# Within a step: node products behind the tasks, node sums behind the weighing, tasks sorted by the age of their inputs

## The chip, the core and the metric

The kernel runs on one core of a Trainium2 chip. A core has five engines with an instruction row each: TensorE (PE, with weight loads PEld), VectorE (DVE), ScalarE (ACT), GpSimd (POOL) and SyncE (SP, which here only issues DMAs). The metric is the device time of a run in microseconds; less is better. The kernel before took 2186.42 us, the median of three runs (2183.76 to 2202.97).

## What is computed

A graph attention layer and a mixture of experts, each added to its input. `x` has 6250 nodes of 256 features, there are 100000 edges, sorted by destination, with destinations denser at low node numbers.

```python
x = x + gnn(layernorm(x), src, dst, ...)      # 8 heads of 32
x = x + moe(layernorm(x), ...)                # 8 experts, the 2 best for each node

# gnn, after a layer norm
h     = xn @ W
e     = leaky_relu(a_src[src] + a_dst[dst], 0.2)
ee    = exp(e - emax[dst])
alpha = ee / segment_sum(ee, dst)[dst]
agg   = segment_sum(h[src] * alpha, dst)
o     = layernorm(agg + xn @ W_res + bias)
return o + gelu_tanh(o @ ffn_w1 + b1) @ ffn_w2 + b2

# moe
top_p, top_idx = top_k(softmax(x @ Wr + br), 2)
y[e] = gelu(layernorm_e(x) @ W1[e] + b1[e]) @ W2[e] + b2[e]
return sum over the two experts of weight * y[expert]
```

## The kernel before

After a first part (to about 150 us) that makes a table `tab_s` of `h` and its attention factors, the kernel runs in **steps**, one loop (L1481 and after) that traces everything by hand: `tc.manual_schedule()` keeps each engine's instructions in the order in which the program emits them. An engine takes its row in that order; what it waits for is a semaphore of another engine or of a DMA.

A step does two things. First it runs the **edge stages** of `STAGES` (L910). Every step `s` fetches four tiles of 128 edges, and the later stages of the pipeline work on what was fetched in earlier steps; a pair `(f, d)` in `STAGES` calls `f(s - d)`:

- `spread` (d=0, DVE, L821 and L828): one-hot of each edge's place in a window of 32 nodes, and the factors `qd`; `turn_spread` (1, PE and ACT, L834, L836) transposes it through the PSUM tile `pt`; `give` (2, PE, L842) gathers destination factors into `pz`.
- `weigh` (3, DVE, L850 to L854): weights and weighted messages `msg` from the gathered `gs` and `pz`; it frees `gs` for the next gathers on POOL (`fetch`, d=0, L812).
- `add_tiles` (4, PE, L869): one-hot times messages, summed in PSUM over a group of steps in `pl`; at the group's end ACT copies it to `part` (L873).
- `place` (4, DVE, L887): at a group's end, a one-hot `oh2` (two buffers) that moves the group's sums to their nodes.
- `add_nodes` (5, PE, L894): the product for nodes, `p2 = oh2 x part`, in a PSUM tile with one buffer (the trace shows it as `p`).
- `sum_up` (6, DVE, L901 and L905): adds `p2` to the nodes' sums `acc_lo` or `acc_hi`, at a place that DVE first loads into a register (`kfi`).

A group has one step in the first 66 steps, where there are few edges for each node, then two steps (31 groups), four (9) and eight (4): 110 groups in 196 steps.

Then the step runs **tasks** (`run_tasks`, L937): pieces of the rest of the work, for units of two node tiles and for blocks of 256 rows of one expert, chosen while each engine has `room` in the step. A task names its engine and its inputs; an input made by another engine must be at least one step old. The PSUM tile `py` has one buffer: a task with `take="py"` can be chosen only when it is free, and a task with `free="py"` chosen earlier in the same step frees it. The tasks spoken of below:

- first units: `wres` (`first_product`, PE, L1147, takes `py`); `rg` (`add_biases`, DVE, L1153 and L1156, frees it).
- node units: `divide` (DVE, L1036 to L1041; its input is an SP load) and `norm_out` (DVE, to L1051); `norm_rows` (ACT); `turn` (PE, L966, through `pt`, and ACT, L973); eight `up` (PE, L981, and ACT, L984); four `down` (PE, L991; the first takes `py`); `add_out` (DVE, L1064); `take_up` (DVE, L1071, frees `py`); `norm_new` (DVE, to L1087); a second `turn`; `logits` (PE, L1113, takes `py`); `choose` (DVE, L1121, frees it).
- for every two units: `mark`, `append`, `rank` (DVE, L1281 to L1296, frees the `py` that `count` took), `enlist`, and scatters (POOL, L1351).
- expert blocks: loads (SP), `note` (DVE, L1417; waits for a buffer that a give-back's DMA has read), `turn`, `up`, `down`, `finish` (DVE, L1426, frees `py`), `weigh_block` (ACT, L1432), give-backs (POOL, L1436).

What a step emits on an engine is thus: the edge stages in the order of `STAGES`, then the tasks in the order in which they were chosen.

Of the kernel before, what the change touches and what calls it, by code (L numbers as in the profile page):

```python
# [218 lines left out]
def gnn_moe_kernel(  # L219
# [47 lines left out]
    while EP < ET:  # L267
        m = 8
        while m > 1:
            gap = 2.0 * N * min(NE, (EP + G * m) * P) / NE ** 2  # L270
# [15 lines left out]
    NG = len(order)  # L286
# [161 lines left out]
    with ExitStack() as actx:  # L448
# [229 lines left out]
        for t0 in range(0, NT, G):  # L678
# [15 lines left out]
            for j in range(n):  # L694
                t = t0 + j
# [91 lines left out]
    def fetch_nodes(c):  # L787

        gq = bw.tile([P, W32 * 2 * H], F32, name="gq", bufs=1)
        nc.gpsimd.indirect_dma_start(  # L790
            out=gq, out_offset=None, in_=tab_q,
            in_offset=bass.IndirectOffsetOnAxis(ap=qrow[:, c:c + 1], axis=0))
        nc.sync.dma_start(tab_g[c * P:(c + 1) * P, :], gq)
        n = min(GC, NQ - c * GC)
        gd = bw.tile([P, GC, 2 * H], F32, name="gd")
        nc.sync.dma_start(gd[:, :n], tab_g[c * P:c * P + n * G, :].rearrange(
            "(g j) (r c) -> (j r) g c", j=G, r=W32))
        gds[c] = gd
# [91 lines left out]
    @behind_group  # L890
    def add_nodes(q):
        part, oh2 = live.pop((q, "part")), live.pop((q, "oh2"))
        p2 = bps.tile([P, DA], F32, name="p2")
        nc.tensor.matmul(p2, oh2, part, start=True, stop=True)  # L894
        live[q, "p2"] = p2

    @behind_group
    def sum_up(q):
# [4 lines left out]
        for b in range(2):  # L903
# [3 lines left out]

    STAGES = ((sum_up, 6), (weigh, 3), (add_tiles, 4), (place, 4), (turn_spread, 1), (give, 2),  # L910
              (spread, 0), (add_nodes, 5), (fetch, 0))
    LASTST = 6


    class Task:
# [3 lines left out]
        def __init__(self, fn, eng, cost, deps=(), take=None, free=None):  # L919
            self.fn, self.eng, self.cost, self.take, self.free = fn, eng, cost, take, free  # L920
            self.deps = []
            for d in deps:
                d, gap = d if isinstance(d, tuple) else (d, None)
                if gap is None:
                    gap = 0 if d.eng == eng == "DVE" else 1
                self.deps.append((d, gap))
            self.step = None

    pending = []
    held = set()  # L930

    def task(*a, **k):
        t = Task(*a, **k)
        pending.append(t)
        return t

    def run_tasks(s, room):  # L937

        more = True
        while more:  # L940
            more = False
            for t in list(pending):
                if (t.take in held or room[t.eng] <= 0.0
                        or any(d.step is None or d.step + gap > s for d, gap in t.deps)):
                    continue
                pending.remove(t)
                t.step = s
                room[t.eng] -= t.cost
                if t.take:
                    held.add(t.take)  # L950
                if t.free:
                    held.remove(t.free)
                t.fn()
                more = True

    def back(tasks, n):

        return tasks[-n:][:1] if len(tasks) >= n else []
# [208 lines left out]
    def first_unit(u):  # L1167
        t0, n, _ = units[u]
        env = {}
        first_loads.append(task(lambda: load_first(t0, n, env), "SP", 0.0,  # L1170
                                [(d, 0) for d in back(firsts, 2)]))
        pr = task(lambda: first_product(n, env), "PE", 0.95 * n, [(first_loads[-1], 2)], take="py")
        ab = task(lambda: add_biases(n, env), "DVE", 0.7 * n,
                  [pr, *[(d, 0) for d in back(firsts, 1)]], free="py")
        firsts.append(task(lambda: store_first(t0, n, env), "SP", 0.0, [ab]))
# [265 lines left out]
    def block_loads(b):  # L1441
        env = {"n": 2}
        needs = next(d for n, d in sure if n > b)
        free = [(d, 0) for d in blocks[b - 2:b - 1] + notes[b - 2:b - 1]] if b >= 2 else []
        env["lw"] = task(lambda: load_weights(b, env), "SP", 0.0,
                         [needs[-1], *([blocks[b - 2]] if b >= 2 else [])])
        env["lx"] = task(lambda: load_block(b, env), "SP", 0.0, [*needs, *free])
        env["lp"] = task(lambda: load_params(b, env), "DVE", 0.4, [needs[-1], *free])
        ahead.append((b, env))

    def block_unit(b, env):
        no = task(lambda: note(b, env), "DVE", 0.6,
                  [(env["lx"], 2), *[(d, 0) for d in back(stored, 3)]])
        dn = net(env, lambda: env["xb"], [(env["lx"], 2), env["lp"]], lambda: env["w"][0],
                 lambda: env["w"][1], AF.Gelu, lambda: env["pc"][:, 0, :],
                 more=[(env["lw"], 2)], scale=lambda: env["pc"][:, 0, KF:])
        fi = task(lambda: finish(env), "DVE", 0.7, [dn, *[(d, 0) for d in back(stored, 2)]],
                  free="py")
        wb_ = task(lambda: weigh_block(env), "ACT", 0.9, [fi, no])
        g0 = task(lambda: give_back(0, env), "POOL", 2.6, [wb_])  # L1460
        stored.append(task(lambda: give_back(1, env), "POOL", 2.6, [g0]))
        blocks.append(fi)
        notes.append(no)
# [15 lines left out]
    s, u, since, was_nodes = 0, 0, [], False  # L1479

    with tc.manual_schedule():  # L1481
        nc.sync.dma_start(xs[E * CAP:, :].rearrange("(p r) d -> p r d", r=2), blank[:, :2])
        while s < NG + LASTST or pending or u < len(units) or len(blocks) < NS:
            for g in range(s, min(s + EARLY, NG)):
                if order[g][0] // GC not in gds:
                    fetch_nodes(order[g][0] // GC)
            for f, d in STAGES:
                if 0 <= s - d < NG:
                    f(s - d)
            if s == NG + LASTST:  # L1490
                edges.close()
            if len(firsts) < len(units) and len(firsts) <= s + 1:
                first_unit(len(firsts))
            if len(firsts) == len(units) and firsts[-1].step is not None and fp:
                first_.close()
                fp = None
            if last_hi and last_hi[0].step is not None and not moew and not fp:
                hi_pool.close()
                moew.append(ctx.enter_context(tc.tile_pool(name="moew", bufs=2, side="right")))
            nb = len(blocks) + len(ahead)  # L1500
            if moew and len(ahead) < 2 and nb < NS and any(n > nb for n, _ in sure):
                block_loads(nb)

            while sum(t.cost for t in pending if t.eng == "PE") < QUEUE:
                if (u < len(units) and units[u][2] <= s - LASTST
                        and not (ahead and was_nodes)):
                    was_nodes = True
                    node_unit(u)
                    since.append(u)
                    u += 1  # L1510
                    if u % 2 == 0 or u == len(units):
                        chunk_tasks(since, u == len(units), u == len(units) - 1)
                        since = []
                elif ahead:
                    was_nodes = False
                    block_unit(*ahead.pop(0))
                else:
                    break
            room = dict(ROOM if s < NG + LASTST else ROOM_AFTER)
            if s < NG + LASTST:  # L1520
                g = s - 5
                ends = 0 <= g < NG and order[g][1] == groups[order[g][0]][1] - 1
                for e in EDGES:
                    room[e] -= EDGES[e] + ends * BEHIND[e]
            run_tasks(s, room)
            s += 1
            if there is None and final_list and final_list[0].step is not None and len(blocks) > NS - 2:
                there = nc.values_load(total[0:1, 0:1], min_val=0, max_val=NB)
        if NS < NB:
            with tc.If(there > NS):  # L1530
                while pending or len(blocks) < NB:
                    nb = len(blocks) + len(ahead)
                    if len(ahead) < 2 and nb < NB:
                        block_loads(nb)
                    if ahead:
                        block_unit(*ahead.pop(0))
                    run_tasks(s, dict(ROOM_AFTER))
                    s += 1
# [31 lines left out]
```

## Time and profile before

| | |
|---|---|
| median of the timed runs | 2186.42 us |
| the profiled execution's own time | 1972.14 us |
| its span, first to last instruction | 1970.4 us |
| mean granted TensorE clock | 0.926 |
| busy: PE, PEld | 1634.8 us (83%), 1250.6 us (63%) |
| busy: DVE, ACT, POOL | 1078.1 us (55%), 707.7 us (36%), 1122.1 us (57%) |
| L894, 220 matmuls (two for each product) | 84.3 us busy, 59.5 us idle of PE before them |
| L905, 220 sums (two for each group) | 108.3 us busy, 106.2 us idle of DVE before them |
| L812, 784 gathers on POOL | 809.9 us busy, 363.9 us idle before them |

Times are those of one profiled execution, which was shorter than the timed runs; durations below are its own. "Busy" is the sum of the instructions' own times; "idle before" is how long the engine stood still just before such an instruction, put down to what ended the wait. A name behind an arrow is the one that was waited for; "issue" means that nothing visible was waited for. A matmul in fp32 appears as two.

### The profile page before, as it was taken

Reading aid. Unit: us, or ns where it says so; the run is one execution under the profiler, and the core shown is the slowest. Engines: PE = TensorE matmul, PEld = TensorE weight load, DVE = VectorE, ACT = ScalarE, POOL = GpSimd, SP = SyncE. Lnnn points to the kernel's source line nnn. Section 1 sums busy time; section 2 is a strip of 40 time slices with the busy share of each in tenths; the row PEclk is TensorE's granted clock in tenths of the full one; section 3 lists DMA queues with packets and bytes.
Section 4 is the critical chain, followed back from the end, with each engine's and each line's share of the span. In section 5 each row is a group of like instructions: output and inputs, shape, how many; then the busy total and the mean of one; then the engine's idle time right before and its main releaser. Section 6 shows DMA issues by size and latency. Waiting matters only on the chain. (4 is left out here: it accounts for less than half of the span.)

```text
span 1970.4 us, 28382 instructions
## 1 busy us (share of the span) xinstructions
PE 1634.8 (83%) x8533; PEld 1250.6 (63%) x8533; DVE 1078.1 (55%) x3964; ACT 707.7 (36%) x1590; POOL 1122.1 (57%) x1165
## 2 busy tenths in 40 slices
PE   4835797778787988999899997996998949999997
PEld 3523565555555766766677765775776737777775
DVE  8836878877878775565667655462453501200000
ACT  3821232322233343344434342433334314333332
POOL 2027765655655767577778777777777722112122
PEclk8968899887887999999999998998999979999999
DMA  4967664644535456566564776576776655565652
GB/s 129 290 210 225 187 202 130 184 134 146 158 112 194 152 152 170 149 199 168 179 200 136 210 206 200 155 220 201 201 232 169 205 184 131 179 186 171 196 161 57
DMA packets 245260, 348.24 MB, mean 177 GB/s; under 512 B 46465, under 2 KB 200353, under 8 KB 245100
## 3 DMA queue, kind: packets, MB, share of 16 engines
q1 hardware_dynamic: 182476, 203.56, 31.8%
q0 software_dynamic: 59312, 139.32, 27.1%
q10 hardware_dynamic: 3312, 3.48, 0.6%
q8 instruction: 70, 1.15, 0.2%
q14 instruction: 90, 0.74, 0.1%
HBM read 282.90 MB, written 67.66 MB: 178 GB/s over the span
## 5 line engine op out<-in xcount | busy, mean ns | idle before, releaser
L812 POOL DMA_INDIRECT gs<-tab_s,srce x784 | 809.9, 1033 | 363.9 <-issue 198.9
L981 PE MATMUL ph<-turned_in,w1b 128*128 128x256 f32 x1696 | 400.3, 390 | 51.2 <-ACT ht L984 38.2
L991 PE MATMUL py<-w2b,ht 128*128 128x256 f32 x1696 | 382.6, 384 | 11.7 <-DVE lg L1121 6.2
L981 PEld LDWEIGHTS ph<-turned_in,w1b 128*128 128x128 f32 x1696 | 305.2, 193 | 124.4 <-ACT ht L984 57.4
L991 PEld LDWEIGHTS py<-w2b,ht 128*128 128x128 f32 x1696 | 325.0, 193 | 58.4 <-DVE lg L1121 7.7
L1436 POOL DMA_INDIRECT out_dram<-yb,to x106 | 176.9, 1668 | 312.5 <-ACT yb L1432 124.5
L984 ACT ACTIVATE ht<-ph,pc 128x256 f32<-128x256 f32 x424 | 198.4, 473 | 206.1 <-PE ph L981 205.6
L854 DVE TENSOR_TENSOR msg<-gs,msg 128x1024 f32<-128x1024 f32 x196 | 240.5, 1227 | 6.7
L1426 DVE TENSOR_TENSOR yb<-py,b2b 128x512 f32<-128x512 f32 x53 | 36.6, 690 | 360.4 <-PE py L991 276.8
L991 PE MATMUL py<-w_sb,ht 128*128 128x256 f32 x784 | 190.5, 405 | 17.3 <-DVE lg L1121 15.0
L981 PE MATMUL ph<-turned_in,w_sb 128*128 128x256 f32 (+1 forms) x800 | 192.5, 394 | 14.2 <-ACT ht L984 14.2
L991 PEld LDWEIGHTS py<-w_sb,ht 128*128 128x128 f32 x784 | 158.7, 205 | 46.4 <-DVE lg L1121 19.6
L981 PEld LDWEIGHTS ph<-turned_in,w_sb 128*128 128x128 f32 x800 | 150.4, 200 | 44.6 <-ACT ht L984 20.3
L873 ACT ACTIVATE part<-pl 128x264 f32<-128x264 f32 x110 | 42.9, 390 | 322.3 <-PE pl L869 319.6
L836 ACT ACTIVATE oht<-pt 128x128 f32<-128x128 f32 x196 | 53.9, 275 | 271.5 <-PE pt L834 214.8
L869 PE MATMUL pl<-msg,oh 128*32 128x264 f32 x1568 | 130.9, 406 | 17.1 <-DVE msg L854 17.0
L1351 POOL DMA_INDIRECT xs<-xe,slot x98 | 103.4, 1055 | 54.3 <-DMA xs<-blank 22.1
L894 PE MATMUL p<-part,oh 128*128 128x264 f32 x220 | 84.3, 469 | 59.5 <-DVE acc_hi L905 38.8
L984 ACT ACTIVATE ht<-ph,prm 128x256 f32<-128x256 f32 (+1 forms) x200 | 92.2, 469 | 113.0 <-PE ph L981 112.6
L834 PEld LDWEIGHTS pt<-ident,oh 128*128 128x128 f32 x196 | 27.6, 141 | 138.3 <-issue 81.0
L834 PE MATMUL pt<-ident,oh 128*128 128x128 f32 x196 | 65.5, 334 | 49.6 <-ACT turned_in L973 23.1
L973 ACT ACTIVATE turned_in<-pt,pc 128x256 f32<-128x256 f32 x106 | 53.9, 559 | 134.4 <-PE pt L966 124.1
(325 smaller groups left out, 1900.8 us busy)
## 6 DMA issues: line engine op xcount, KB each, us to landing
w1b<-in_L_ffn_W_dram SPq DMA_DIRECT2D x53, 1024.0 KB
w2b<-in_L_ffn_W_dram SPq DMA_DIRECT2D x53, 1024.0 KB
xb<-xs SPq DMA_DIRECT2D x53, 260.0 KB
gs<-tab_s,srce POOLq DMA_INDIRECT x784, 3.3
b2b<-in_L_ffn_b_dram SPq DMA_DIRECT2D x53, 128.0 KB
tab_s<-hg SPq DMA_DIRECT2D x12, 544.0 KB
xg<-in_x_dram SPq DMA_DIRECT2D x12, 512.0 KB
xt_d<-xt SPq DMA_DIRECT2D x12, 512.0 KB
```

The lines of the kernel that those rows point to most:

```text
L812: nc.gpsimd.indirect_dma_start(out=gs[:, j, :], out_offset=None, in_=tab_s, in_offset=bass.IndirectOffsetOnAxis(ap=srce[:, t:t + 1], axis=0))
L834: nc.tensor.transpose(po[:, 0, :P], live[s, "oh"].rearrange("p j r -> p (j r)"), ident)
L836: nc.scalar.activation(oht, po[:, 0, :P], AF.Copy)
L854: nc.vector.tensor_tensor(msg[:, :, :D].rearrange("p t (h d) -> p t h d", h=H), gs[:, :, :D].rearrange("p t (h d) -> p t h d", h=H), msg[: ...
L869: nc.tensor.matmul(pl[j * W32:(j + 1) * W32, :], oh[:, j, :], msg[:, j, :], start=i == 0, stop=last)
L894: nc.tensor.matmul(p2, oh2, part, start=True, stop=True)
L973: nc.scalar.activation(xt[:, k, :n * P], pt[:, k, :n * P], AF.Identity, bias=scale[:, KD + k:KD + k + 1], scale=scale[:, k:k + 1])
L981: nc.tensor.matmul(ph[:, :W], w1[:, k, c * P:(c + 1) * P], env["in"][:, k, :W], start=k == 0, stop=k == KD - 1)
L984: nc.scalar.activation(ht[:, :W], ph[:, :W], func, bias=b[:, c:c + 1], scale=1.0)
L991: nc.tensor.matmul(env["py"][:, j, :], env["ht", c][:, j * P:(j + 1) * P], w2[:, c, :], start=c == 0, stop=c == KF - 1)
L1351: st = nc.gpsimd.indirect_dma_start(out=xs, out_offset=bass.IndirectOffsetOnAxis(ap=slots[k][:n, t:t + 1], axis=0), in_=xes[u // 2][:n, pl ...
L1436: nc.gpsimd.indirect_dma_start(out=out, out_offset=bass.IndirectOffsetOnAxis(ap=env["to"][:, j:j + 1], axis=0), in_=env["yb"][:, j, :], in ...
```

## The change

Three edits, all in what a step emits in which order. No instruction is added or taken away by them.

1. `STAGES` no longer has `add_nodes`; the loop calls `add_nodes(s - 5)` after the step's tasks.
2. `sum_up` moves from the head of `STAGES` to behind `spread`.
3. `run_tasks` still chooses tasks in the same way, but emits them only when all are chosen, sorted by `late`: 0 for a task without an input from the last step (an SP load never counts), 1 for a task with one. A task takes over the `late` of an input of the same step, and of the task that freed the PSUM tile that it takes, if that was in the same step. The sort keeps the order of equals.

```diff
-    STAGES = ((sum_up, 6), (weigh, 3), (add_tiles, 4), (place, 4), (turn_spread, 1), (give, 2),
-              (spread, 0), (add_nodes, 5), (fetch, 0))
+
+    STAGES = ((weigh, 3), (add_tiles, 4), (place, 4), (turn_spread, 1), (give, 2), (spread, 0),
+              (sum_up, 6), (fetch, 0))
     LASTST = 6
...
             self.step = None
+            self.late = 0
 
     pending = []
     held = set()
+    freed = {}
...
     def run_tasks(s, room):
 
-        more = True
+
+        chosen, more = [], True
         while more:
...
                 pending.remove(t)
                 t.step = s
+                t.late = max([d.late if d.step == s else int(d.step == s - 1 and d.eng != "SP")
+                              for d, gap in t.deps], default=0)
                 room[t.eng] -= t.cost
                 if t.take:
                     held.add(t.take)
+                    t.late = max(t.late, freed.get(t.take, (None, 0))[1] * (
+                        freed.get(t.take, (None, 0))[0] == s))
                 if t.free:
                     held.remove(t.free)
-                t.fn()
+                    freed[t.free] = s, t.late
+                chosen.append(t)
                 more = True
+        for t in sorted(chosen, key=lambda t: t.late):
+            t.fn()
...
             run_tasks(s, room)
+            if 0 <= s - 5 < NG:
+                add_nodes(s - 5)
             s += 1
```

What this makes of some steps (`s` is the loop's counter; PE's stages L869, L834, L842 stand ahead of every PE row, `weigh`, `place` and `spread` ahead of every DVE row, except that in the kernel before `sum_up` stands ahead of them):

```
step  engine  before                                       after
31    PE      add_nodes, down x4                           down x4, add_nodes
31    DVE     choose, divide, norm_out                     sum_up, divide, norm_out, choose
38    PE      add_nodes, wres, up x5                       wres, up x5, add_nodes
38    DVE     rg, append, divide, norm_out                 sum_up, divide, norm_out, rg, append
39    PE      add_nodes, count, turn, up x3                up x3, count, turn, add_nodes
71    PE      down x4                                      down x4
71    DVE     choose, divide, norm_out                     sum_up, divide, norm_out, choose
77    PE      up x3, turn, count                           up x3, turn, count
77    DVE     finish, divide, norm_out                     sum_up, divide, norm_out, finish
```

## Prediction

> **What bounds the kernel now.** I read first the busy shares in 40 slices of the span (49 us each), then the idle time before instructions by releaser, stretch by stretch, then the timeline where the moved instructions lie.
>
> ```profile
> PE 4835797778787988999899997996998949999997
> DVE 8836878877878775565667655462453501200000
> POOL 2027765655655767577778777777777722112122
> ```
>
> The digits are tenths. The edge steps run from about 150 to 1575 us. I cut them where the limits change. Stage A, to about 640 us: the 66 groups of one step each, so every step has a product for nodes and a sum (L894, L905). PE and DVE both sit near 8 tenths, neither full. Stage B, to about 950 us: PE at 9 tenths. Stage C, to 1570 us: a table by stretch gives PE 557.30 and POOL 480.46 us busy of 620. POOL's waits there are nearly all its fixed 0.3 us between issues (93.7 us before 311 gathers, 15 more before other DMAs); 480 and some 110 plus small waits fill the 620, so POOL sets the pace in C. Stage D, from 1660 us, is blocks on PE alone.
>
> Waits of PE and DVE from 200 to 640 us (total us, times, longest):
>
> ```profile
> PE p L894 <- DVE acc_hi L905: 38.5, 15, 5.3
> PE p L894 <- DVE acc_lo L905: 16.4, 5, 7.1
> PE py L991 <- DVE lg L1121: 10.5, 7, 2.2
> DVE xin L1071 <- PE py L991: 20.4, 6, 5.0
> DVE acc_hi L905 <- PE p L894: 12.7, 4, 4.4
> DVE acc_hi L905 <- issue: 12.3, 19, 1.0
> DVE acc_lo L905 <- issue: 3.2, 5, 0.7
> ```
>
> PE waits 54.9 us for a sum to free `p`, which looks like the thing to remove. But DVE, which it waits for, stood still for PE only some 35 us of these 440, so at most that much can come back through it. How the two interlock shows in the timeline around a step with `down` (DVE, then PE):
>
> ```profile
> 333.57 0.22 DVE L1121 SCALAR_TENSOR_TENSOR lg<-py,rr,br_bc 128x8 f32<-128x8 f32 x1
> 334.78 0.23 DVE L1036 RECIPROCAL rd<-acc_hi 128x16 f32<-128x16 f32 x1
> 340.33 0.16 DVE L1051 SCALAR_TENSOR_TENSOR nm<-mvc,rc 128x2 f32<-128x2 f32 x1
> 341.18 1.02 DVE L905 SCALAR_TENSOR_TENSOR acc_hi<-p,here,acc_hi 128x264 f32 x2 [0.68 <-issue]
> 344.26 0.68 DVE L1071 TENSOR_TENSOR xin<-xin,py 128x512 f32<-128x512 f32 x1
> ```
> ```profile
> 334.44 7.17 PE L991 MATMUL py<-w_sb,ht 128*128 128x256 f32 x32 [2.17 <-DVE lg L1121]
> 417.19 9.62 PE L991 MATMUL py<-w_sb,ht 128*128 128x256 f32 x32 [1.64 <-DVE lg L1121]
> ```
>
> `choose` (L1121) reads the last of `py` and lets `down` start; `divide` and `norm_out` (L1036 to L1051, 5.7 us), a sum and a weighing run on DVE under the 7.17 us of `down`; `take_up` (L1071) then finds it done. The second PE line is the same product after PE had stood 4.76 us and then 1.64 us: 9.62 us.
>
> **What the Trainium skill says.** "PSUM — Partial Sum Buffer", Engine vs sequencer instructions: DVE, ACT and GpSimd take instructions strictly first in, first out, and matmuls stay in program order. The trace agrees: 20 times PE stands at L894 with its tasks queued behind. So a wait put into DVE's row holds every task behind it. "TensorE: Matmul & The Clock Gate", What's actually happening: PE's clock is halved until activity releases it, after an idle window of about 3.4 us. The trace agrees in kind: 7.17 against 9.62 us. "ScalarE: Activation LUTs", What ACT_TABLE_LOAD costs: about 1283 ns; the trace has 1283.
>
> **The change, part by part.** In the order of the instructions of the two built programs every task stays in its step, and POOL's row is the same line for line.
>
> Moved: 110 products (a pair of 0.66 us, 0.5 us of PE's row) behind PE's tasks; 110 sums (two of 0.49 us) behind weigh, place and spread. The work is the same; the waits are not. `place`'s one-hot (L887, two buffers) takes the buffer that the product of the step before read, and the sum needs the same product. Both therefore now wait for the END of PE's previous step. Queued behind on DVE: spread, `qd`, the sum, all tasks; for those wait PE's `py` products, ACT and, a step later, POOL's gathers.
>
> Stage A, by walking the timeline with the durations of the trace:
> 1. The gap before the sum in which DVE loads a register (15.5 us in 24 steps, <-issue) is hidden behind the 1.22 us weighing now ahead of it: -16.
> 2. `take_up` after `down`: now product 0.5, semaphore 0.1, place to `qd` 0.53 (343.73 to 344.26), sum 0.93 (341.18 to 342.11) lie between: 2.0 us, 11 times: +22.
> 3. The sort calls `divide` not late (its input is an SP load), and `choose` or `rg`, which free `py`, late (inputs from PE's last step). In steps 16, 21, 26 and 31 the freer now comes 5.7 us later, and so does `down`; its cover, those same 5.7 us, is gone. For the step shown: the freer ends at 339.6, `down` at 346.8 (warm) or 349.2 (cold), `take_up` near 349 or 351 instead of 344.3. Less item 2 that is +2.7 to +5; I take 4, four times: +16.
> 4. Same sort elsewhere: step 38 (`wres` and five `up` behind a late `rg`, 5.5), 41 (`add_out` before `choose`, 1.4), 54 (1.5): +8.
> 5. Other steps in which PE's previous step is the longer (`up` x7 after `take_up`, about 1 us; six of them): +6.
> PE's 54.9 us at L894 I count as nothing: PE then waits for the `py` freers instead. Sum of A: +36.
>
> Stage B: DVE is ahead of PE, so after each closing step its tasks begin 1.6 us into PE's step. Where PE's first `py` product needs a freer of the same step, PE stands for 1.6 plus the DVE work ahead of the freer and the freer itself, less the 0.9 us of PE's own edge products: step 71 7.2 (`divide`, `norm_out`, `choose`), 77 5.1, 89 and 103 1.9 each (`note` ahead of `choose`), 91 and 105 2.1 each (`append` ahead of the rank): 20.3, of which 2.7 are waited in 91 and 105 today. Against that: turns placed last now often have a product (0.5 us) before the next `pt` (L834 <- L973 waits 18.5 us over B and C; I take 4 in B), and 3.3 us at L894. With one more table load (58 against 57) 17.6-7.3+1.3, and a little of it taken up by POOL's 26 us of waits for DVE there: +10.
> SP: in twelve places loads of `xin` and `res` go ahead of stores or of `xb`; two loads (under 1 us) later for the others, covered by the two-step lead of the loads. Nothing.
> Stage C: nothing; PE has 63 us of slack there, DVE more, POOL's row is unchanged. If that cover failed, B's kind of wait would add up to 10.
> Stage D: `turned_in` before `up` (0.66 us, 15 times): in half the blocks the turn now goes before the `down` of the block before: -5.
>
> Sum: 36+10+0-5 = +41. The profiled execution took 1972.14 us (span 1970.4): it would take 2013. The timed runs (2183.76 to 2202.97) are 214 us longer than it, which no view explains; I add the 41 to the median of 2186.42 unscaled (scaled: 45): **2227 us**.
>
> No row shows the new wait at L887. Below: 0, if PE always finishes first; a wait by itself gains nothing. Above: each of the 66 steps held 2 us, 132. The walk (items 2, 3 and 5, 44 us in 66 steps) gives 0.7 a step; that stands.
>
> **Rivals.** (a) Forecast, 0.50: +20 to +60. (b) A wash, 0.23: PE's earlier start of tasks that are not late returns what items 2 to 5 take, and C swallows the rest; -10 to +15, about 2190. For it: 54.9 us of PE waits; against: PE is not what A ends on. (c) Faster, 0.12, by one mechanism at L894: the wait there lets PE cool (1.25 us for a 0.66 pair, 9.62 for 7.17). If PE, no longer held, does its `down` earlier in at least half the steps, the 20.4 us at L1071 and the 12.7 us at L905 go, with the 16 us of item 1: about -35, 2151. It decides where DVE's waits on PE from 200 to 640 us fall below some 20 us. Against: `down` needs `py`, which DVE frees. (d) Worse, 0.15: `note` (L1417), which waits for a give-back's DMA (116.1 us, 17 times, up to 16.9), is now traced ahead of `finish` and, in some eight steps, of `choose`; five such waits of 8 us in front of `down`, on top of (a): +81, 2267. For it: such a wait already cost PE 10.2 us at 1226 us; against: C has slack.
> That the edit does not do what it says is excluded by the instruction order.
>
> **Numbers.** 1% is 22 us, about what this measurement can tell from no change. (a) lies above it in nine tenths; (b) almost all within; (c) below in nine tenths. Slower 0.45+0.15+0.02, same 0.05+0.21+0.01, faster 0.11. The range leaves out the far ends of (c) and (d): 2165 to 2275; (a) alone 2206 to 2246.
>
> **What would show it.** L894 waits for DVE almost gone; L1071 no longer waiting on L991, but L887 waiting on L894, 30 to 60 us in A; `py <- lg` (10.5) and `py <- rg` (11.9) grown; PEclk in A not higher; POOL <- msg grown before 640 us; C as long as now. The forecast is wrong if DVE's waits on PE in A are not longer than today's 35 us, or if C stretches.

## The result and the profile after

The changed kernel takes 2256.07 us, median of 4 runs (2250.06 to 2268.71), against 2188.78 (2183.76 to 2202.97, 4 runs) for the kernel before: ratio 1.0304, 95% interval 1.0238 to 1.037, slower by 67 us. The forecast was +41 (2227), in a range of 2165 to 2275.

Two levels have to be kept apart. In the comparisons below the kernel before takes about 1976 us on one chip ("the quick chip") and about 2185 us on two others, some 10% more. The profile shown ahead of the prediction (1972.14 us) is at the quick level, the times of the result are at the other. So the changed kernel's profile (2250.06, span 2248.3) is set below beside a second one of the kernel before at the slower level (2191.19, span 2189.4), and each experiment's time beside the kernel before in the same comparison.

The busy shares in 40 slices, in tenths of a slice. The kernel before at this level (55 us a slice):

```profile
PE   4844787776776787879797887887887887999997
DVE  8835678776677464554656354445343341120000
POOL 2047555564546556565666665757666542122112
```

After (56 us a slice):

```profile
PE   5734677567767788878788787888687976999997
DVE  8835656676777655455646444435343341220000
POOL 1056443546545655565556556666656561121222
PEclk8966888788787898989989898999898987999999
```

In slices 4 to 13, about stage A, neither PE nor DVE exceeds 7 after the change; both reach 8 before it. In stage C (slices 20 to 33) POOL is mostly at 5 or 6 in both: the row of sevens by which the prediction said that POOL sets the pace there belongs to the quick level.

The groups of the moved work: busy time, mean ns of one, then the idle time of the engine ahead of it and what ended it. Before, at this level:

```profile
L894 PE MATMUL p<-part,oh 128*128 128x264 f32 x220 | 85.2, 473 | 48.5 <-DVE acc_hi L905 23.4 <-DVE acc_lo L905 12.8 <-issue 12.4
L905 DVE SCALAR_TENSOR_TENSOR acc_lo<-p,here,acc_lo 128x264 f32 x112 | 55.2, 493 | 121.5 <-PE p L894 66.7 <-issue 20.0 <-PE ph L981 16.7
L905 DVE SCALAR_TENSOR_TENSOR acc_hi<-p,here,acc_hi 128x264 f32 x108 | 53.1, 492 | 73.7 <-PE p L894 20.6 <-remote 16.1 <-issue 12.7
L887 DVE TENSOR_SCALAR oh<-jrow,snloc 128x128 f32<-128x128 f32 x110 | 30.8, 280 | 0.0
```

After:

```profile
L894 PE MATMUL p<-part,oh 128*128 128x264 f32 x220 | 76.6, 433 | 19.2 <-DVE acc_hi L905 11.6 <-DVE acc_lo L905 7.3 <-issue 0.3
L905 DVE SCALAR_TENSOR_TENSOR acc_lo<-p,here,acc_lo 128x264 f32 x112 | 55.1, 492 | 183.2 <-PE p L894 91.4 <-remote 24.0 <-PE py L1002 21.9
L905 DVE SCALAR_TENSOR_TENSOR acc_hi<-p,here,acc_hi 128x264 f32 x108 | 53.1, 491 | 8.9 <-issue 7.0
L887 DVE TENSOR_SCALAR oh<-jrow,snloc 128x128 f32<-128x128 f32 x110 | 31.5, 286 | 141.4 <-PE p L894 95.4 <-issue 17.2 <-PE ph L992 14.1
```

Place's one-hot (L887) had no wait at all before; now DVE stands 141.4 us ahead of it, 95.4 of them for the product that closes PE's previous step. Ahead of the one-hot and the sum together it stands 333.5 us, against 195.2. ("remote" is a wait whose releaser the profile does not name.)

Waits of stage A by engine (total us, times, longest), each from the weighing of step 9 to that of step 69. Before, 194 to 708 us:

```profile
DVE acc_hi L905 <- PE p L894: 20.6, 5, 8.4
DVE acc_hi L905 <- issue: 12.7, 20, 1.0
PE py L1147 <- DVE rg L1153: 20.5, 7, 10.2
PE py L991 <- DVE lg L1121: 5.9, 4, 2.0
```

After, 195 to 760 us (lines of the tasks stand 11 lower: L991 is now L1002, L1071 L1082, L1121 L1132, L1147 L1158, L1153 L1164):

```profile
DVE oh L887 <- PE p L894: 95.4, 22, 8.3
DVE acc_hi L905 <- issue: 6.8, 31, 0.6
PE py L1158 <- issue: 56.3, 11, 10.2
PE py L1002 <- DVE lg L1132: 39.5, 9, 12.1
```

Each engine now stands for the other: DVE 95.4 us for the product, PE 39.5 us for `choose` (`lg`, 5.9 before) and 56.3 us ahead of `wres`. That last wait has no releaser in the profile ("issue"), but the timeline gives it: all eleven end 0.10 us after the end of a DVE instruction that frees `py`, eight times the bias sum `rg` (51.5 us) and three times `take_up` (4.7 us). So it is in the main the wait for `rg` (20.5 us before), under another name.

The step that the prediction walked through looks like this after the change (start, duration, engine, and in brackets the idle time ahead and its releaser):

```profile
400.97 0.25 DVE L1047 RECIPROCAL rd<-acc_hi 128x16 f32<-128x16 f32 x1
406.29 0.16 DVE L1062 SCALAR_TENSOR_TENSOR nm<-mvc,rc 128x2 f32<-128x2 f32 x1
406.98 0.21 DVE L1132 SCALAR_TENSOR_TENSOR lg<-py,rr,br_bc 128x8 f32<-128x8 f32 x1
417.64 0.28 DVE L887 TENSOR_SCALAR oh<-jrow,snloc 128x128 f32<-128x128 f32 x1 [8.30 <-PE p L894]
419.41 0.68 DVE L1082 TENSOR_TENSOR xin<-xin,py 128x512 f32<-128x512 f32 x1
```
```profile
407.24 9.92 PE L1002 MATMUL py<-w_sb,ht 128*128 128x256 f32 x32 [12.12 <-DVE lg L1132]
417.00 0.61 PE L894 MATMUL p<-part,oh 128*128 128x264 f32 x2
```

`divide` and `norm_out` (400.97 to 406.45) now stand ahead of `choose`. PE waits 12.12 us for it and comes back at the halved clock, as "TensorE: Matmul & The Clock Gate" of the Trainium skill (What's actually happening) has it after an idle window: the granted clock is 0.50 to 412 us and 1.00 from 414 us, and `down` takes 9.92 us instead of 7.17. In the four steps of item 3 `down` takes 9.43, 8.97, 10.19 and 9.92 us, against 7.07 to 7.17 in both profiles of the kernel before: 10 us of the loss there are this clock. Under `down` DVE has only a weighing left, reaches `place` and stands 8.30 us for the product behind `down`.

**Where the loss lies.** The start of each weighing (L850, 196 in all) marks the steps. Difference to the kernel before at the same level, in us: A is step 3 to 69, B 69 to 105, C 105 to 198, D from there to the end. The second column is another profile of the changed kernel (experiment 9), the third is the changed kernel with a third one-hot buffer on the quick chip (experiment 5).

```
        after      after again   with 3 buffers (quick chip)   forecast
start    +1.5         -1.1          -2.3                            0
A       +50.5        +54.8         +42.6                          +36
B        -8.5         +0.3          +4.4                          +10
C       +16.0        +22.2         +13.8                            0
D        -0.7         -4.1          -4.0                           -5
total   +58.9        +72.2         +54.5                          +41
```

A single profile leaves some room in such a table: steps 8, 14 and 54 are 8.4 to 9.8 us longer in the second profile of the kernel before than in the first, with no change of the program.

### The profile page after: what moved, and what is told of

It reads as the page before. It is cut to its first block, busy times and chain, and to the rows that moved or that the text cites. A ratio compares the mean times of both kernels' runs of the same rounds, so it can differ in the third digit from the quotient of the medians.

```text
span 2248.3 us, 28319 instructions
## 1 busy us (share of the span) xinstructions
PE 1723.6 (77%) x8533; PEld 1302.1 (58%) x8533; DVE 1083.0 (48%) x3964; ACT 704.0 (31%) x1591; POOL 1093.3 (49%) x1165
## 5 line engine op out<-in xcount | busy, mean ns | idle before, releaser
L812 POOL DMA_INDIRECT gs<-tab_s,srce x784 | 787.6, 1005 | 595.9 <-DVE msg L854 282.0
L992 PE MATMUL ph<-turned_in,w1b 128*128 128x256 f32 x1696 | 424.9, 403 | 91.6 <-ACT ht L995 49.1
L992 PEld LDWEIGHTS ph<-turned_in,w1b 128*128 128x128 f32 x1696 | 315.7, 200 | 176.2 <-ACT ht L995 74.0
L1002 PE MATMUL py<-w2b,ht 128*128 128x256 f32 x1696 | 393.9, 392 | 21.0 <-DVE lg L1132 12.3
L1002 PEld LDWEIGHTS py<-w2b,ht 128*128 128x128 f32 x1696 | 331.3, 198 | 69.6 <-DVE lg L1132 13.3
L1002 PE MATMUL py<-w_sb,ht 128*128 128x256 f32 x784 | 200.3, 419 | 60.2 <-DVE lg L1132 43.1
L992 PE MATMUL ph<-turned_in,w_sb 128*128 128x256 f32 (+1 forms) x800 | 205.6, 410 | 44.1 <-ACT ht L995 39.6
L1002 PEld LDWEIGHTS py<-w_sb,ht 128*128 128x128 f32 x784 | 164.7, 213 | 88.8 <-DVE lg L1132 45.0
L869 PE MATMUL pl<-msg,oh 128*32 128x264 f32 x1568 | 141.6, 432 | 20.8 <-issue 10.7
L850 DVE TENSOR_TENSOR ww<-gs,pz 128x64 f32<-128x64 f32 x196 | 43.0, 219 | 208.3 <-PE pz L842 96.5
L905 DVE SCALAR_TENSOR_TENSOR acc_lo<-p,here,acc_lo 128x264 f32 x112 | 55.1, 492 | 183.2 <-PE p L894 91.4
L1158 PE MATMUL py<-wres,xtf 128*128 128x256 f32 x196 | 74.8, 548 | 70.0 <-issue 56.6
L834 PEld LDWEIGHTS pt<-ident,oh 128*128 128x128 f32 x196 | 28.6, 146 | 158.8 <-issue 108.6
```

The lines of the kernel that those rows point to most:

```text
L812: nc.gpsimd.indirect_dma_start(out=gs[:, j, :], out_offset=None, in_=tab_s, in_offset=bass.IndirectOffsetOnAxis(ap=srce[:, t:t + 1], axis=0))
L850: nc.vector.tensor_tensor(ww, gs[:, :, D:], live.pop((s, "pz")).rearrange("p (j c) -> p j c", j=G), op=ALU.mult)
L869: nc.tensor.matmul(pl[j * W32:(j + 1) * W32, :], oh[:, j, :], msg[:, j, :], start=i == 0, stop=last)
L905: nc.vector.scalar_tensor_tensor(to, p2, here[:, b, q:q + 1], to, op0=ALU.mult, op1=ALU.add)
L992: nc.tensor.matmul(ph[:, :W], w1[:, k, c * P:(c + 1) * P], env["in"][:, k, :W], start=k == 0, stop=k == KD - 1)
L1002: nc.tensor.matmul(env["py"][:, j, :], env["ht", c][:, j * P:(j + 1) * P], w2[:, c, :], start=c == 0, stop=c == KF - 1)
```

## The experiments

All lines of edits are against the kernel before or the changed kernel, as named.

**1. The kernel before again.**

> The kernel before, unchanged, profiled once more. Its first profiled execution took 1972 us while its timed runs took 2184 to 2203; the changed kernel's profiled execution (2250) lies at its timed level. If that first profile was an unusually undisturbed execution, this one comes out near 2190, with a granted clock of about 0.88 instead of 0.926, and stages A, B and C are longer than in the first profile; then the waits of the two kernels are to be compared with this one. If the profile by itself shortens this kernel, it comes out near 1972 again.

2191.19 us, clock 0.886: the first alternative. In the three comparisons that follow, the kernel before took 2185.94 us (16 runs), 1975.72 (24 runs) and 2184.81 (36 runs). So the 214 us which the prediction could not explain are not an effect of profiling; they are as large as the difference between the two levels. (On which chip the first profile was taken is not on record.) Against the first profile, stages A, B and C are 57, 55 and 119 us longer, and D is 13 us shorter.

**2. Only the sort.** The tasks as the changed kernel sorts them; `STAGES` as before:

```
+        for t in sorted(chosen, key=lambda t: t.late):
+            t.fn()
```

> The kernel before with only the late sort of the tasks; products for nodes and sums stay where they were. My theory (the sort puts the tasks that free py behind divide and norm_out; items 3 and 4 and half of B): about +25 to +35 us, with PE's waits for lg and rg at py longer by some 20 us, and no waits of DVE at the one-hot of place. Rival theory (all of the loss comes from the moved product, through place and the sum waiting for the end of PE's step): -10 to +10 us. Rival theory (the sort is good by itself): faster by over 10 us.

1.0122 (1.0094 to 1.015), +27 us: as expected. The trace has no wait at L887. PE's waits for DVE at `py` from 200 to 640 us are 57.9 us in all, against 33.4: 24.5 more, where some 20 were expected. (Two of them, 15.1 us, are put down to the last instruction of `norm_out`, but they end 0.05 us after the bias sum `rg` behind it.)

**3. Only the move.** The changed kernel with

```
-        for t in sorted(chosen, key=lambda t: t.late):
+        for t in chosen:
```

> The changed kernel with the tasks of a step traced in the order in which they are chosen, as before: only the products and sums are moved. My theory (the new wait at the one-hot and the sum costs items 2 and 5 and half of B, less item 1): about +20 to +35 us against the kernel before, with 60 us or more of DVE waits at L887 for the product of the previous step. If the sort carries the loss: within 10 us of the kernel before. If the moved product carries it all: +55 to +75.

1.0122 (1.0071 to 1.0172), +31 us between the medians: as expected. From 200 to 640 us:

```profile
DVE oh L887 <- PE p L894: 58.0, 18, 7.5
```

Each half costs about as much; together they cost 67, some ten more than the sum, which is within the intervals.

**4. Only the product.** The product behind PE's tasks, the sum still at the head of DVE's step, no sort:

```
-    STAGES = ((sum_up, 6), (weigh, 3), ..., (spread, 0), (add_nodes, 5), (fetch, 0))
+    STAGES = ((sum_up, 6), (weigh, 3), ..., (spread, 0), (fetch, 0))
...
             run_tasks(s, room)
+            if 0 <= s - 5 < NG:
+                add_nodes(s - 5)
```

> Only the product for nodes is moved behind PE's tasks; the sum stays at the head of DVE's step, no sort. The sum at the head then waits for the end of PE's previous step, ahead of the weighing and of all else, so that the gathers' buffers and the messages come later too. If the wait of DVE on the end of PE's step is the mechanism, this is the worst of the forms: +60 to +120 us. If the loss lies in the sort or in the place of the sums: within 15 us of the kernel before.

1.0612 (1.056 to 1.0665): +138 us, above even the upper end. The same two engines, the same work; only the first thing that DVE meets in a step is now the end of PE's last one. From step 9 to step 69:

```profile
DVE acc_hi L905 <- PE p L894: 110.6, 23, 9.3
PE py L1158 <- issue: 53.8, 13, 8.8
```

In the kernel before, the first of these is 20.6 us. This is the clearest case for the wait of DVE on the END of PE's step. Experiment 3 has the same product and the sum behind the weighing and the spread: there the wait holds up less.

**5. A third one-hot.** The changed kernel with

```
-        oh2 = bw.tile([P, P], F32, name="oh2")
+        oh2 = bw.tile([P, P], F32, name="oh2", bufs=3)
```

> The changed kernel with three buffers for the one-hot of place instead of two, so that place no longer waits for the product at the end of PE's previous step; the sum, which needs that product, still does, with one short one-hot and qd between. My theory (the wait is for the end of PE's step, wherever it stands in DVE's row): the DVE wait moves from L887 to L905 nearly whole, and the time stays within 10 us of the changed kernel's 2256. If the second buffer itself is what costs: 25 us or more faster than that.

On the quick chip: 2025.23 us against 1975.72, 1.0244 (1.0213 to 1.0275). The changed kernel itself was not run on this chip, so the gain is known only as far as the intervals go (1.0304 and, below, 1.0362 on the others). Put on the 2188.78 us of the result, 1.0244 is 2242, which decides neither for "within 10 us" of 2256 nor for "25 us or more faster". The waits moved as the theory says; L887 has none, and the sum has them:

```profile
L905 DVE SCALAR_TENSOR_TENSOR acc_lo<-p,here,acc_lo 128x264 f32 x112 | 55.0, 491 | 114.9 <-PE p L894 112.2 <-issue 0.7
L905 DVE SCALAR_TENSOR_TENSOR acc_hi<-p,here,acc_hi 128x264 f32 x108 | 53.0, 491 | 93.8 <-PE p L894 91.9
```

Those of `acc_hi` lie in stage A (157 to 601 us): 91.9 us for the product, where the changed kernel stood 95.4 us at L887. In all the sum stands 208.7 us, against 106.2 in the kernel before at the quick level. The buffer of `place` is only the first place where DVE meets the end of PE's step; take it away, and DVE stands at the sum.

**6 and 7. The sum behind the tasks, with and without the sort.** Three one-hot buffers, `sum_up` out of `STAGES`, and

```
             run_tasks(s, room)
+            if 0 <= s - 6 < NG:
+                sum_up(s - 6)
             if 0 <= s - 5 < NG:
                 add_nodes(s - 5)
```

> The changed kernel with three one-hot buffers and the sum behind DVE's tasks instead of ahead of them: nothing in DVE's row ahead of the tasks needs the end of PE's previous step any more; the late sort stays. My theory: the moved part of the loss (about 30 us) and the part that only sort and move make together (about 10) go, the sort's remains: 2200 to 2220. If the wait of DVE on PE's end is harmless and PE's later start is the cause: no gain, 2245 or more.

> The same as the run before this one, without the late sort: product and sum behind the tasks of their engines, three one-hot buffers. My theory: neither the freers are demoted nor do DVE's tasks wait for the end of PE's step, and PE's wait at L894 and the register load are out of the way: 2165 to 2195, at best faster than the kernel before. If moving the product costs PE by itself: 2205 or more.

With the sort 1.0063 (1.0048 to 1.0078), without it 1.001 (0.9997 to 1.0023). Put on the 2186 us of the slower chips, 2200 and 2188: both about as expected, though the second beats nothing. DVE's tasks no longer have anything ahead of them that needs PE's end, and the loss of the move is gone (the third buffer and the new place of the sum come together here; by experiment 5 the buffer alone leaves most of the wait). PE's wait for the sum is not gone; from 200 to 640 us, without the sort:

```profile
PE p L894 <- DVE acc_hi L905: 54.7, 21, 6.8
PE p L894 <- DVE acc_lo L905: 13.7, 5, 6.5
```

68.4 us, more than the 54.9 of the kernel before, at the same total time. So 13.5 us more of this wait, the most visible of the first profile, cost nothing. What its removal would bring is not shown: no run removes it alone.

**8. The freers left where they were.** In the sort of the changed kernel:

```
-int(d.step == s - 1 and d.eng != "SP")
+int(d.step == s - 1 and d.eng != "SP" and not t.free)
```

> The changed kernel whose sort no longer counts a task that frees the py bank as late on account of a product of PE's last step, so that choose, rank, finish and the bias sum keep their place ahead of divide and norm_out. My theory (items 3 and 4: the sort costs by demoting the freers): most of what the sort costs goes, 20 to 35 us faster than the changed kernel, 2220 to 2236, and the PE waits for lg at py in A fall from 37 us to under 15. If the sort costs by the order of PE's own tasks: within 10 us of 2256.

On the quick chip 1.0149 (1.0109 to 1.0188), against 1.0244 with the sort as it is (experiment 5, which differs in the third buffer too): 18 us between the two medians, just below the expected 20 to 35. PE's waits for `lg` ahead of `down` from 200 to 640 us are 23.2 us against 38.4; under 15 was expected. By step, in us more than the kernel before at the same level (one step is from a weighing to the next; the first four rows are of the quick level, the last two of the other):

```
step                        17     22     27     32     39     42     55
3 buffers (experiment 5)    6.6    6.0    5.5    6.7    5.3    1.8    1.4
sum behind tasks, sort      6.6    6.1    4.8    4.8    3.2    1.3    0.5
sum behind tasks, no sort   0.1    0.2    0.0   -0.1    0.0   -0.6    0.0
freers not late             8.2    1.5   -0.5    2.0    1.2    1.6    0.0
sort only (experiment 2)    6.2    3.1    4.1    5.8    4.4    0.1    1.2
move only (experiment 3)    0.2   -0.2    0.6   -0.2    0.9   -0.2    0.0
```

These are the seven steps of items 3 and 4 (16, 21, 26, 31, 38, 41, 54; the delay shows in the step behind). The sort makes this part without the move, and the move does not make it (last two rows). Keeping the freers early takes most of it away in five of the steps, and not in 17 and 42; why not there is open.

**9. The changed kernel again**, in one comparison with the next three:

> The changed kernel once more, in one comparison with the next three, so that its stages can be set beside a profile of the kernel before of the same speed. My theory: 1.024 to 1.034 of the kernel before; the loss is made between the steps 9 and 45 (stage A), where DVE waits 80 to 110 us for the end of PE's step, and stage B adds nothing.

2268.96 us, 1.0362 (1.027 to 1.0454), a little above what was expected. Between steps 9 and 45 it loses 57 us (the first profile of it: 49), DVE waits 99.3 us in A for the product, and B adds 0.3 us, as expected; C adds 22.2.

**10. Only item 1.** The kernel before with one edit:

```
-    STAGES = ((sum_up, 6), (weigh, 3), (add_tiles, 4), ...
+    STAGES = ((weigh, 3), (sum_up, 6), (add_tiles, 4), ...
```

> The kernel before with one edit: the sum behind the weighing of its step, the product where it was, no sort. Item 1 of the prediction alone: the 15 us of waits for the register load in A go below 7 us. My theory: the product at the head of PE's step now waits 1.8 us longer for the sum, which puts PE's tasks back by as much, but DVE is what A ends on: 0 to 12 us faster than the kernel before. If PE's start is what counts: 5 to 20 us slower.

2163.07 us against 2184.81: 0.9862 (0.9779 to 0.9944). It beats both kernels, by more than expected between the medians (22 us); the interval reaches from 12 to 48 us. The sum, in the whole span:

```profile
L905 DVE SCALAR_TENSOR_TENSOR acc_lo<-p,here,acc_lo 128x264 f32 x112 | 54.8, 489 | 2.7 <-issue 0.7
L905 DVE SCALAR_TENSOR_TENSOR acc_hi<-p,here,acc_hi 128x264 f32 x108 | 52.9, 490 | 5.1 <-remote 1.6 <-PE ph L981 0.5 <-issue 0.2
```

7.8 us of waits, against 195.2 in the kernel before at this level (121.5 and 73.7). So more than the register load is covered; the reading is that the weighing no longer queues behind a sum that waits for PE. PE's wait for the sum grows from 36.2 to 44.3 us without a loss, as in experiment 7. Part of the old wait turns up ahead of the weighing (338.1 us, from 179.2), so the net gain is far smaller than 187 us.

**11 and 12. The register early, without and with a sort that spares the freers.** Experiment 7 with the register load taken out of `sum_up` and put behind the weighing; then with the sort of experiment 8:

```
+    STAGES = ((weigh, 3), (load_k, 6), (add_tiles, 4), ...
```

> Product and sum behind the tasks, three one-hot buffers, no sort (the run that came out at 1.001 of the kernel before), and the register of the sum loaded behind the weighing, some microseconds before the sum. My theory: the 15.7 us of waits for the register load in A nearly go: 8 to 18 us faster than the kernel before. If those gaps lie beside waits for PE anyway: within 4 us of it.

> The run before this one with the late sort, but with the tasks that free the py bank not counted as late on account of PE's last step. My theory: the sort's loss lay in the demoted freers, so that it is within 5 us of the run without a sort. If the order of PE's own tasks costs as well: 8 us or more slower than that run. If calling late tasks last is worth something once the freers are left alone: 5 us or more faster.

Without the sort 0.9922 (0.9889 to 0.9956), 13 us faster than the kernel before, as expected: in A the sum has no wait put down to "issue" (16.3 us in experiment 7, which ran on another chip). With the sort 1.0034 (1.0008 to 1.006), 23 us slower than without it: a miss. In A the two are alike (-16.6 us each at step 69); the second loses 12 us between steps 93 and 111 and, after winning 4 back, 8 more from 171 to 195. In the first stretch lie two waits of PE for `lg`, 13.5 and 12.9 us, which are 4.6 and 5.9 us without the sort; DVE itself stands 10.6 and 10.8 us ahead of these `choose`, for something that the profile does not name. So sparing the freers mends the sort in A and not later; by what the sort costs there is not settled.

## Why the prediction was right, and where it was not

**Direction and mechanism.** Right, by its own steps. `place` and the sum wait for the end of PE's step (141.4 us at L887, none before); experiment 4 shows the wait alone, experiment 7 a form in which no task of DVE stands behind it, and which has no loss. The sort demotes the freers: the table by step shows it in the steps that were named, and not without the sort.

**The size** was too small, and that it lies in the range is in part luck. +67 us is more than the +20 to +60 of forecast (a), and 2256 is above its own 2206 to 2246. The range went on to 2275 for the sake of rival (d), which did not come about; what filled it is in stages A and C.

**Stage A, item by item.** Item 1: the idle time ahead of the sum put down to "issue" fell from 16.5 us to 7.8, 9 us rather than 16; experiment 10 shows that the edit is worth more by itself. Items 3 and 4, with the 2.0 us a step of item 2 in the four steps of item 3, were 16 + 8 + 8 = 32; measured 24.7 + 8.5 = 33.3 on the quick chip, from whose level they were worked out, and 30.1 + 11.3 = 41.4 at the level of the times. The remaining items were to give +4 (36 - 32), and gave +9.3 and +9.1. So at the level of its own profile the walk through the timeline was good to 7 us (as far as the third buffer changes nothing); adding it unscaled to a time of the other level was the first mistake. The same step, 32, costs 6.7 us there and 7.9 here. Scaled by the ratio of the times, the total would have been 45; items 3 and 4 grew more than that. The move alone (experiment 3) makes A 24.8 us longer in its profile, where items 1, 2 and 5 give 12: the parts of the walk are less sure than their sum.

**PE's wait at L894 counted as nothing:** nothing speaks against it; it grew by 13.5 us in experiment 7 and by 8.1 in experiment 10 without a loss.

**Stages B and C** were mis-sized most: +10 and 0 were forecast, and B gave -8.5, +0.3 and +4.4, C +16.0, +22.2 and +13.8. In B the six waits of PE that were listed came, in the steps that were named: 16.9, 15.3 and 17.6 us in the three profiles of the table above, against 20.3; step 71 alone 7.2, 6.2 and 6.5, against 7.2. But B did not grow by that much. The step that failed is the sum of B, which let every wait of PE lengthen the stage; what takes them up is open.

In C, "PE has 63 us of slack there ... POOL's row is unchanged" rested on POOL setting the pace. At the level of the times it doesn't: from step 105 to 198 POOL waits 132.8 us for DVE (81.5 for `oh`, 51.3 for `msg`) in the kernel before, against 12.4 in the profile that the prediction read. That is not the whole of it, as C stretched by 13.8 us on the quick chip too. The kind of wait that was bounded at "up to 10" arrived: PE's waits for DVE at `py` in C grew from 3.3 us to 13.0 and 18.8 in the two profiles after, and from 7.0 to 13.3 on the quick chip. That is 6 to 8 us short of the stretch in each; and in experiment 7 these waits did not grow (6.2 us) and C still was 6.7 us longer. No run takes these waits away alone, so the cause of C's stretch stays open.

**Stage D:** -5 forecast, -0.7 to -4.1 found.

**The rivals.** (c) needed DVE's waits on PE in A below 20 us; they are above 100. (The three terms put down for it, 20.4, 12.7 and 16, make 49 and not about 35.) (d), `note` held up ahead of `choose`, is in neither profile of the changed kernel; it was seen once, on the quick chip with three buffers:

```profile
1597.60 0.35 DVE L1428 COPY to<-xb 128x2 int32<-128x2 int32 x1 [4.02 <-DMA out_dram<-yb,to]
1598.07 0.22 DVE L1132 SCALAR_TENSOR_TENSOR lg<-py,rr,br_bc 128x8 f32<-128x8 f32 x1
```
```profile
1598.94 1.65 PE L1002 MATMUL py<-w2b,ht 128*128 128x256 f32 x3 [4.61 <-DVE lg L1132]
```

`note` stands 4.02 us for the DMA, and PE 4.61 us for the `choose` behind it: such a wait can hold up PE, but it came once and not five times, at half of the 8 us.

**What was to be seen.** L894's waits fell to 19.2 us, L1071's are gone from A, `lg` grew, POOL's waits for `msg` from step 9 to 69 rose from 155.9 to 205.8 us, and PE's clock in A is not higher (0.75, 0.78 and 0.80 in the stretches 150 to 300, 300 to 450 and 450 to 640 us, against 0.77, 0.88 and 0.79). L887's 95.4 us are well over the 30 to 60, and `rg` grew only under the name "issue". C stretched by 16 and 22 us (steps 105 to 198), which the prediction had named as a sign that it was wrong: for that stage it was.

## What to carry to other kernels

Where two engines take turns, moving an operation to the end of one engine's step costs nothing in work but ties whatever needs it, its result or only its operand's buffer, to that END: ask what now stands first in the other engine's row that needs it, and put such an operation behind the work that doesn't. A rule that emits late tasks last must not demote the ones that free a shared bank; sparing them mended the first stage here, and not the later ones. A wait added to an engine need not lengthen its stage: the waits forecast for B came, and B did not grow by them. And whether "another engine sets the pace" has to be read at the level of the run whose time is forecast; a profile from a quicker chip does not show it.

## What had not been expected of the hardware

The same program took 1975.72 us (24 runs) and 2184.81 us (36 runs) in comparisons on two different chips, with a granted clock of 0.92 to 0.93 in the runs of the one and 0.88 to 0.90 in those of the other. In the two profiles of the kernel before, POOL's idle time ahead of its gathers was 363.9 us and 589.2 us; a gather itself was no slower (1033 and 1003 ns). Stage D, PE alone, was no slower at the slower level either (experiment 1): the difference lies in the stages with edges. Its cause is open; each chip was in one comparison only, so chip and hour are not told apart.

A register load ahead of the sum costs up to 1.0 us of DVE's time when it opens a step (12.7 us in 20 steps of A), 0.2 us a step behind `spread` (6.8 us in 31 steps), and next to nothing directly behind a weighing of 1.22 us (0.2 us in all of A, experiment 10). That the gap is the load is seen in experiment 11: the load was moved, and the gap is gone.
